# Attention biases made ahead and kept in DRAM, and one of four PSUM copies moved to VectorE, in a four-layer gated transformer

## Chip, core and metric

The kernel runs on one core of a Trainium2 chip. The metric is device time in microseconds for one execution. Three runs of the kernel before took 1968.76, 1974.26 and 1973.82 us, median 1973.82.

## What is computed

The input `x` holds 16 batches of 128 tokens with 256 features (float32). Four layers follow each other; each adds a gated cross-attention over a context and then a gated feed-forward part. The change touches the feed-forward part of layer 0, which sends each token to one of eight experts, and the attention of layer 1, which adds a bias to the scores and masks them:

```python
# layer 0, feed-forward: one expert per token
routing_indices = jnp.argmax(router_logits, axis=-1)
for e in range(E):
    g, u = xe @ gate_w[e].T, xe @ up_w[e].T          # 704 wide
    out = out + jnp.where(mask, (silu(g) * u) @ down_w[e].T, 0.0)
# layer 1, attention: 16 heads of width 16
scores = (Q @ K.T + relative_time) * HEAD_DIM ** (-0.5)
scores = jnp.where(attn_mask, scores, -jnp.inf)       # one mask and one bias per batch, all heads
attn = jnp.nan_to_num(softmax(scores), nan=0.0)       # rows without any key give zero
out = (attn @ V) @ Wout.T + bout
```

`relative_time` is `rel` in the kernel (16 x 128 x 128 float32, 64 KB a batch), `attn_mask` is `mask` (a byte per element, 16 KB a batch).

## The kernel before

Tokens lie on the 128 partitions, one tile `xb[b]` per batch. Each layer's attention is a software pipeline over the 16 batches: in step t, a list of stages (`stages`, L693 on, for the masked layer) is gone through in order, and a stage with lag k works on batch t - k. Within this pipeline the order of instructions on TensorE (PE), VectorE (DVE), ScalarE (ACT) and GpSimd (POOL) is that of the list (`manual_schedule`). SyncE's (SP) queue of DMAs, and everything outside such a block, is ordered by the scheduler.

One step of the masked attention, by its parts:

- `scores` puts 16 heads' products into four PSUM banks (TensorE). `maxima` (L543, L555) adds the batch's bias to each head's scores and takes the negated row maximum, 16 operations on VectorE, each writing an SBUF tile `e`; the first 12 stand ahead of `normalise` in the list, the last 4 behind it.
- `exps` (L572) takes 16 exponentials with row sums on ScalarE, for the batch one step earlier; four of them open the step, twelve follow after three small copies.
- `normalise` (L578) inverts the sums (L580) and multiplies by a 0/1 factor for rows without a key (L582), both on VectorE, and GpSimd scales the four tiles (L585).
- `turn` (L591) transposes the probabilities of a batch into four PSUM banks `pe`; `take_turned` (L597) copies the four to SBUF. In the masked layer all four copies are on ScalarE, behind the exponentials. In the layers without a bias two of the four are on VectorE.
- Behind them come the products with the values and the output projection, `add` (L265, VectorE), and for the feed-forward part the router's logits: `red` (their maximum, L1146, VectorE) and `lg` (their exponential, L1147, ScalarE), which stands on ScalarE ahead of the next step's exponentials. It works on the batch eight steps back, so that the first steps have none.

The bias comes from `attention1` (L1811). `load` fetches a batch's mask and `rel` (L1817, L1819); `mask` turns the bytes into 0 or -2^100 on GpSimd (L1824); `make` takes the row maximum of that (L1830), compares it (L1831), and forms 0.25 rel + mask in place (L1832), all on VectorE. Three buffers each.

Layer 0's experts are `sorted_experts` (L891). `Routing.solve` sorts the tokens by expert; its last result is `used` (L888, GpSimd), the number of blocks of 128 tokens that are needed. The usual 20 blocks are run in a straight line; a branch on `used` (L1014, L1019) runs up to three more ahead of them if needed, and every engine takes that branch for itself. Per block, GpSimd gathers the weights (2.2 MB, L904) and the tokens (128 KB), the weights three blocks ahead in four buffers; TensorE transposes the tokens (L216), multiplies (L938); ScalarE takes the SiLU (L943), VectorE the product `h` (L944); TensorE transposes `h` (L954) and multiplies again (L969); VectorE copies the result `y` (L973), GpSimd scatters it (L974). The blocks are outside of `manual_schedule`. While they run, SyncE has nothing to do until it loads the next attention's weights (L137).

Of the kernel before, what the change touches and what calls it, by code (L numbers as in the profile page):

```python
# [12 lines left out]
F32 = mybir.dt.float32  # L13
# [3 lines left out]
ALU = mybir.AluOpType  # L17
AX = mybir.AxisListType

P = 128  # L20
B, S, D = 16, 128, 256
# [3 lines left out]
HUGE = 2.0 ** 100  # L25
# [6 lines left out]
FEW0 = B * S // P + 4  # L32
# [4 lines left out]
def flamingo_gated(ctx: ExitStack, tc: tile.TileContext, a, out):  # L37
    nc = tc.nc

    const = ctx.enter_context(tc.tile_pool(name="const", bufs=1))  # L40
# [29 lines left out]
    def gate_f(layer):  # L70
# [10 lines left out]
        out=before, in_=ones, compare_op=ALU.is_gt, fill=0.0, base=0, pattern=[[1, P]], channel_multiplier=-1  # L81
# [16 lines left out]
    part = const.tile([P, 1], F32, name="part")  # L98
# [14 lines left out]

    normed = [tc.dram_tile([B * S, D], F32, name=f"normed{i}") for i in range(2)]
    spill = tc.dram_tile([B, P, 2048], F32, name="spill")
    results = [tc.dram_tile([(2 * B + n) * S, D], F32, name=f"results{i}") for i, n in enumerate((NBLK0, NBLK1))]

    def load_slot(src, cols, name, queue=nc.sync):
# [298 lines left out]
    def xattn16(layer, bias=None, after=None, joining=None, draining=None):  # L417
# [7 lines left out]
        after, logits, take_logits, choose = after  # L425
        with ExitStack() as es:
# [198 lines left out]
            def add(b):  # L625
                add_gated(b, outs.pop(b)[:, 0:D], gate_x(layer))

            added, masks, turning = {}, {}, {}
            bias_load = bias_mask = bias_make = None
            if bias is not None:  # L630
                bias_load, mask, make = bias

                def bias_mask(b):
                    masks[b] = mask(b)

                def bias_make(b):
                    added[b] = make(b, masks.pop(b))

            def turn_norm(b):
                turning[b] = bank("pt")  # L640
# [16 lines left out]
            def part(stage, *args):  # L657
                return lambda b: stage(b, *args)


            if bias is None:
                stages = (
                    (4, part(exps, (0,))),
                    (3, value_rows),
                    (1, norm.take),
                    (8, after.take),
                    (6, take_heads),
                    (4, part(exps, (1, 2, 3))),
                    (-1, join),
                    (-1, norm.stats),  # L670
                    (7, after.stats),
                    (None, project),
                    (3, take_values),
                    (5, turn),
                    (5, part(take_turned, nc.vector.tensor_copy, (0, 2))),
                    (0, norm.apply),
                    (7, after.apply),
                    (0, output_bias),
                    (None, mask_keys),
                    (9, choose),  # L680
                    (8, logits),
                    (6, output),
                    (8, take_logits),
                    (4, normalise),
                    (6, add),
                    (5, part(take_turned, nc.scalar.copy, (1, 3))),
                    (None, part(project, True)),
                    (3, scores),
                    (3, part(maxima, range(4))),
                    (0, turn_norm),  # L690
                    (7, turn_after),
                    (5, values),
                    (None, draining),  # L693
                )
            else:
                stages = (
                    (1, bias_load),
                    (2, bias_mask),
                    (3, scores),
                    (4, part(exps, (0,))),  # L700
                    (1, norm.take),
                    (8, after.take),
                    (6, take_heads),
                    (4, part(exps, (1, 2, 3))),
                    (7, after.stats),
                    (-1, join),
                    (-1, norm.stats),
                    (9, choose),
                    (2, bias_make),
                    (3, value_rows),  # L710
                    (None, project),
                    (0, norm.apply),
                    (7, after.apply),
                    (0, output_bias),
                    (None, mask_keys),
                    (3, part(maxima, (0, 1, 2))),
                    (5, turn),
                    (8, logits),
                    (6, output),
                    (4, normalise),  # L720
                    (3, part(maxima, (3,))),
                    (3, take_values),
                    (6, add),
                    (5, part(take_turned, nc.scalar.copy, range(4))),
                    (None, part(project, True)),
                    (8, take_logits),
                    (0, turn_norm),
                    (7, turn_after),
                    (5, values),
                    (None, draining),  # L730
                )
# [156 lines left out]
            nc.gpsimd.tensor_copy(self.used, end[:, 15:16])  # L888
            fillers[3]()

    def sorted_experts(routing, src, inter, few, first, lead=None, last=None):  # L891


        layer, nblk = routing.layer, routing.nblk
# [4 lines left out]
        with ExitStack() as es:  # L899
# [81 lines left out]
            def blocks(first, last):  # L981

                for t in range(first - 1, last + 1):
                    if first + 3 <= t + 3 < last:
                        load(t + 3)
                    if first <= t < last:
                        gate_up(t, cuts[0])
                    if first <= t - 1 < last:
                        turn_hidden(t - 1)
                    if first <= t + 1 < last:  # L990
                        turn_tokens(t + 1)
                    if t < first and behind is not None:
                        behind()
                        load(2)
                    if first <= t < last:
                        for cut in cuts[1:]:
                            gate_up(t, cut)
                    if first <= t - 1 < last:
                        down(t - 1)

            weights[0] = first
            with tc.manual_schedule(engines=ENGINES):
# [77 lines left out]
    def attention_ffn0():  # L1080
        with tc.tile_pool(name="r0", bufs=1) as rp:
            wr = rp.tile([P, 2, 8], F32, name="wr0")
            nc.sync.dma_start(out=wr, in_=a["rw0"])
            routing = Routing(0, rp, 1, NBLK0, wr)
            vals = [rp.tile([P, 16], F32, tag=f"lg{i}", name=f"lg{i}") for i in range(2)]
            for t in vals:
                nc.gpsimd.memset(t, SENT)

            turned = {}

            def into(b):
                turned[b] = rp.tile([P, 2, P], F32, tag="rT", name="rT", bufs=2)
                return turned[b]

            products = {}

            def logits(b):
                products[b] = routing.logits(b, turned.pop(b))

            def take_logits(b):  # L1100
                nc.vector.tensor_copy(vals[b % 2][:, 0:8], products.pop(b))

            first = []

            def choose(b):
                if b == 4:
                    first.append(load_slot(a["we0"][0], a["we0"].shape[2], "we0"))
                routing.choose(b, vals[b % 2])

            attention0((Norm(into, store=normed[0]), logits, take_logits, choose))  # L1110
            routing.solve()
            sorted_experts(routing, a["we0"], 704, FEW0, first[0])
        return results[0], 1, lambda i, b: gate_f(0)

    def attention_ffn1(joining):
# [694 lines left out]
    def attention1(after, joining, draining):  # L1810
        load_attention(1)  # L1811
        with tc.tile_pool(name="rel", bufs=3) as rp:
            loaded = {}

            def load(b):
                m = rp.tile([P, S], a["mask"].dtype, tag="m", name="m")
                nc.sync.dma_start(out=m, in_=a["mask"][b])  # L1817
                r = rp.tile([P, S], F32, tag="r", name="r")
                nc.sync.dma_start(out=r, in_=a["rel"][b])  # L1819
                loaded[b] = m, r  # L1820

            def mask(b):
                mf = rp.tile([P, S], F32, tag="mf", name="mf")
                nc.gpsimd.tensor_scalar(mf, loaded[b][0], -1.0, HUGE, ALU.add, ALU.mult)  # L1824
                return mf

            def make(b, mf):
                r = loaded.pop(b)[1]
                f = rp.tile([P, 1], F32, tag="f", name="f")
                nc.vector.tensor_reduce(f, mf, AX.X, ALU.max)  # L1830
                nc.vector.tensor_scalar(f, f, -1.0, None, ALU.is_ge)  # L1831
                nc.vector.scalar_tensor_tensor(r, r, 0.25, mf, ALU.mult, ALU.add)  # L1832
                return r, f

            xattn16(1, (load, mask, make), after, joining, draining)

    def attention3(after):
        wa = load_slot(a["wqk3"], 4096, "wqk3", nc.gpsimd)
# [117 lines left out]
```

## Time and profile before

| | |
|---|---|
| median of three runs | 1973.82 us (1968.76 to 1974.26) |
| profiled execution | 1967.84 us, span 1966.1 us, mean TensorE clock 0.977 |
| layer 0's experts | 187.6 to about 371 us of the span |
| masked attention of layer 1 | first maxima at 388.2, last round of four copies at 543.95 |
| exponentials there (L572) | 256, mean 403 ns, and 256 reads of the sum, mean 202 ns |
| scaling on GpSimd there (L585) | 64, mean 1070 ns |
| mask on GpSimd (L1824) | 16, mean 297 ns |
| bias on VectorE (L1830, L1831, L1832) | 16 each, mean 282, 154 and 282 ns |

The profile names an engine, a line, the operation, the output and the inputs, then busy microseconds and the mean of one instruction in nanoseconds; behind that stands how long the engine stood idle just before, and what ended it. In a timeline the columns are start, duration, engine, line and operation, and in brackets the idle time and its releaser. In a table of stretches each engine's busy time is given with its number of instructions, then TensorE's granted clock (1.00 is full speed), the share of time in which the 16 DMA engines were busy, and GB/s.

### The profile page before, as it was taken

How to read it: one execution, taken by the hardware profiler on the slowest of the kernel's cores; microseconds unless marked ns; L12 is line 12 of the kernel's file. 1: busy time of each engine (PE TensorE's matmuls, PEld its weight loads, DVE VectorE, ACT ScalarE, POOL GpSimd, SP SyncE). 2: the span in 40 equal slices, each digit the busy share in tenths (PEclk: the TensorE clock that was granted, in tenths of full speed). 3: DMA queues.
4: the chain of work that ended last, by engine and by line, in shares of the span. 5: the costliest groups of instructions: out<-in, count | busy, mean ns of one | idle time of the engine just before them, and what ended most of it. 6: DMA issues, size and time to landing. Idle time of an engine off the chain costs nothing. (4 is left out here: it accounts for less than half of the span.)

```text
span 1966.1 us, 31038 instructions
## 1 busy us (share of the span) xinstructions
PE 1820.7 (93%) x10345; PEld 1217.5 (62%) x10345; DVE 1253.9 (64%) x3715; ACT 923.0 (47%) x3047; POOL 806.8 (41%) x972
## 2 busy tenths in 40 slices
PE   7996999978889999999989999889999999999897
PEld 4774566556646666656754444367866777775776
DVE  4885222389762222249979999989927666673797
ACT  5993222399931222239951121244524434443874
POOL 5863332377510454438842222211002222230796
PEclk9997999999999999999999999989999999999899
DMA  5002787510000788861002414643200000000000
GB/s 169 15 18 85 293 299 274 168 34 26 18 19 31 259 312 317 310 230 36 2 28 91 169 77 171 239 173 129 87 0 1 1 1 1 23 1 1 7 17 22
DMA packets 53138, 204.21 MB, mean 104 GB/s; under 512 B 11760, under 2 KB 31728, under 8 KB 42224
## 3 DMA queue, kind: packets, MB, share of 16 engines
q0 software_dynamic: 13584, 117.32, 16.3%
q1 hardware_dynamic: 38752, 84.87, 12.3%
q8 instruction: 84, 1.38, 0.3%
q14 instruction: 78, 0.64, 0.1%
q10 hardware_dynamic: 640, 0.00, 0.0%
HBM read 171.75 MB, written 30.41 MB: 103 GB/s over the span
## 5 line engine op out<-in xcount | busy, mean ns | idle before, releaser
L938 PE MATMUL pg<-we,xT 128*128 128x512 f32 (+1 forms) x520 | 237.3, 586 | 0.6 <-ACT xT L217 0.6
L585 POOL TENSOR_TENSOR e<-e,sums 128x512 f32<-128x512 f32 x192 | 198.9, 1067 | 69.3 <-DVE sums L582 31.8
L944 DVE TENSOR_TENSOR h<-sg,pg 128x256 f32<-128x256 f32 x132 | 54.3, 411 | 225.5 <-ACT sg L943 225.5
L572 ACT ACTIVATE e<-sc,mx 128x128 f32<-128x128 f32 x512 | 181.3, 422 | 16.3 <-DVE mx L550 15.2
L943 ACT ACTIVATE sg<-pg 128x256 f32<-128x256 f32 x132 | 49.5, 375 | 278.6 <-PE pg L938 277.4
L356 POOL TENSOR_TENSOR e<-e,rec 128x512 f32<-128x512 f32 x64 | 65.2, 1039 | 228.4 <-DVE rec L355 145.8
L938 PEld LDWEIGHTS pg<-we,xT 128*128 128x128 f32 x520 | 94.0, 192 | 78.2 <-issue 69.9
L904 POOL DMA_INDIRECT we<-in_we,rows x54 | 51.6, 956 | 213.3 <-PE pd L969 151.6
L572 ACT ACTIVATION_READ_ACCUMULATOR e<-sc,mx 128x1 f32 x512 | 134.0, 262 | 0.0
L1425 PE MATMUL acc<-d,k 128*128 128x512 f32 x256 | 120.6, 615 | 11.5 <-POOL d L1415 11.1
L591 PE MATMUL pe<-ident,e 128*128 128x128 f32 x768 | 105.1, 280 | 28.1 <-DVE mx L555 14.1
L1415 POOL TENSOR_TENSOR d<-d,tot 128x1024 f32<-128x1024 f32 x32 | 62.6, 1957 | 164.6 <-DVE tot L1414 153.8
L969 PE MATMUL pd<-we,hT 128*128 128x256 f32 x520 | 125.3, 383 | 1.2 <-ACT hT L958 1.2
L1410 ACT ACTIVATE d<-d 128x1024 f32<-128x1024 f32 x32 | 33.8, 1057 | 186.7 <-DVE d L1409 174.2
L969 PEld LDWEIGHTS pd<-we,hT 128*128 128x128 f32 x520 | 96.9, 190 | 39.2 <-issue 22.9
L1513 PE MATMUL po<-yt,cT 128*128 128x256 f32 x512 | 120.9, 380 | 0.0
L1246 PE MATMUL pl<-phi,xnT 128*128 128x512 f32 x256 | 115.2, 593 | 1.6 <-DVE lg L1402 1.6
L591 PEld LDWEIGHTS pe<-ident,e 128*128 128x128 f32 x768 | 86.4, 142 | 47.0 <-POOL e L585 23.7
L200 POOL TENSOR_SCALAR ve<-mv 128x1 f32<-128x1 f32 (+1 forms) x136 | 30.3, 223 | 206.9 <-DVE mv L207 172.1
L572 ACT ACTIVATE e<-e,mx 128x128 f32<-128x128 f32 x256 | 99.2, 403 | 0.3 <-DVE mx L555 0.3
L1513 PEld LDWEIGHTS po<-yt,cT 128*128 128x128 f32 x512 | 92.4, 190 | 10.1
L1425 PEld LDWEIGHTS acc<-d,k 128*128 128x128 f32 x256 | 48.3, 195 | 76.5 <-issue 53.9
(315 smaller groups left out, 4363.0 us busy)
## 6 DMA issues: line engine op xcount, KB each, us to landing
spill<-lg SPq DMA_DIRECT2D x32, 512.0 KB, 3.0
ew<-in_ew SPq DMA_DIRECT2D x8, 2048.0 KB
cw<-spill SPq DMA_DIRECT2D x14, 1024.0 KB, 13.1
got<-results SPq DMA_DIRECT2D x48, 128.0 KB, 1.9
normed<-xn SPq DMA_DIRECT2D x32, 128.0 KB, 2.5
aw<-in_aw SPq DMA_DIRECT2D x6, 512.0 KB
ws<-in_we SPq DMA_DIRECT2D x2, 1536.0 KB, 6.4
we<-in_we SPq DMA_DIRECT2D x1, 2176.0 KB
```

The costliest lines, as they stand in the source:

```text
L356: nc.gpsimd.tensor_tensor(e, e, rec.unsqueeze(2).to_broadcast([P, 4, S]), ALU.mult)
L572: nc.scalar.activation(e[:, c, :], sc[:, c, :], AF.Exp, bias=mx[:, h : h + 1], scale=sign, accum_out=sums[b][:, h : h + 1],)
L585: nc.gpsimd.tensor_tensor(e, e, r, ALU.mult)
L591: nc.tensor.transpose(pe[:, c * P : (c + 1) * P], e[:, c, :], ident)
L904: nc.gpsimd.indirect_dma_start(out=out, out_offset=None, in_=of, in_offset=bass.IndirectOffsetOnAxis(ap=rows[:, j : j + 1], axis=0),)
L938: nc.tensor.matmul(pg[:, 0 : 2 * m].rearrange("p (g i) -> p g i", g=2), lhsT=tokens[j][:, k, :], rhs=wgu[:, k, :, i0 : i0 + m], start=(k = ...
L944: nc.vector.tensor_tensor(hidden[j][:, i0 : i0 + m], sg[:, 0:m], pg[:, m : 2 * m], ALU.mult)
L969: nc.tensor.matmul(pd[:, 0:D], lhsT=hT[0:m, ic, :], rhs=wd[0:m, ic, :], start=(ic == 0), stop=(ic == nic - 1))
L1246: nc.tensor.matmul(pl, lhsT=xnT[b // 4][:, k, (b % 4) * S : (b % 4 + 1) * S], rhs=tables[0][:, k, n], start=(k == 0), stop=(k == 1),)
L1415: nc.gpsimd.tensor_tensor(dv, dv, tot.unsqueeze(2).to_broadcast([P, 32, 32]), ALU.mult)
L1425: nc.tensor.matmul(acc[hf][k][q], lhsT=keep[b][:, k * P : (k + 1) * P], rhs=d[:, q * 512 : (q + 1) * 512], start=(b == 0), stop=(b == B - 1),)
L1513: nc.tensor.matmul(pos[b][:, 0:D], lhsT=cT[:, c, :], rhs=yt[2 * q + c // 2][:, c % 2, :], start=(q == 0 and c == 0), stop=(q == 3 and c == 3),
```

## The change

The biases are no longer made in the masked attention. `attention_ffn0` hands `sorted_experts` a function `beside`, which is called once at the end of each of the blocks 0 to 16: it issues the loads of batch t's mask and `rel`, makes batch t - 1's bias on VectorE (the mask too, which was on GpSimd), and stores it to a DRAM tile `biases`; the 0/1 factors stay in SBUF in `some`. `attention1` then loads one 64 KB tile per batch. And the first of the four copies of turned probabilities in the masked layer is on VectorE, between the 0/1 factor and the last four maxima.

```diff
+    biases = tc.dram_tile([B, P, S], F32, name="biases")
+    some = const.tile([P, B], F32, name="some")
...
-                    (2, bias_mask),
...
                     (4, normalise),
+                    (5, part(take_turned, nc.vector.tensor_copy, (0,))),
                     (3, part(maxima, (3,))),
                     (3, take_values),
                     (6, add),
-                    (5, part(take_turned, nc.scalar.copy, range(4))),
+                    (5, part(take_turned, nc.scalar.copy, (1, 2, 3))),
...
                     if first <= t - 1 < last:
                         down(t - 1)
+                    if beside is not None and first == 0 and t >= 0:
+                        beside(t)
...
+            with tc.tile_pool(name="rel", bufs=3) as bp:
+                given = {}
+                def beside(t):
+                    if t < B:
+                        m = bp.tile([P, S], a["mask"].dtype, tag="m", name="m")
+                        nc.sync.dma_start(out=m, in_=a["mask"][t])
+                        r = bp.tile([P, S], F32, tag="r", name="r")
+                        nc.sync.dma_start(out=r, in_=a["rel"][t])
+                        given[t] = m, r
+                    if 0 <= t - 1 < B:
+                        m, r = given.pop(t - 1)
+                        mf = bp.tile([P, S], F32, tag="mf", name="mf", bufs=2)
+                        nc.vector.tensor_scalar(mf, m, -1.0, HUGE, ALU.add, ALU.mult)
+                        f = some[:, t - 1 : t]
+                        nc.vector.tensor_reduce(f, mf, AX.X, ALU.max)
+                        nc.vector.tensor_scalar(f, f, -1.0, None, ALU.is_ge)
+                        nc.vector.scalar_tensor_tensor(r, r, 0.25, mf, ALU.mult, ALU.add)
+                        nc.sync.dma_start(out=biases[t - 1], in_=r)
+                sorted_experts(routing, a["we0"], 704, FEW0, first[0], beside=beside)
...
-                m = rp.tile([P, S], a["mask"].dtype, tag="m", name="m")
-                nc.sync.dma_start(out=m, in_=a["mask"][b])
-                r = rp.tile([P, S], F32, tag="r", name="r")
-                nc.sync.dma_start(out=r, in_=a["rel"][b])
-                loaded[b] = m, r
...
+                loaded[b] = rp.tile([P, S], F32, tag="r", name="r")
+                nc.sync.dma_start(out=loaded[b], in_=biases[b])
...
+            def make(b):
+                return loaded.pop(b), some[:, b : b + 1]
```

The order that the scheduler gives VectorE around the branch in the built program, shortened (the lines are those of the changed kernel; `mf`, `some`, `r` are the bias of one batch):

```text
L881  expert<-past                      end of the routing
L1127 mf, L1129 some, L1131 r, L1130 some        batch 0, waits for its loads
L1127 mf, L1129 some, L1131 r, L1130 some        batch 1
...
L1127 mf, L1129 some                             batch 8
L1015 used, L1020 CompareAndBranch
...
L1130 some, L1131 r                     batches 8 and 7
L1127 mf, L1129 some, L1131 r           batch 9, sum of batch 8
...
L943  h<-sg,pg                          first block's first product
```

On the other engines the order of instructions is otherwise as it was, but for the masks that leave GpSimd and the copy that leaves ScalarE.

More of the change, by code (lines that the diff above doesn't have):

```diff
@@ L626, in add @@
                 add_gated(b, outs.pop(b)[:, 0:D], gate_x(layer))
-            added, masks, turning = {}, {}, {}
-            bias_load = bias_mask = bias_make = None
+            added, turning = {}, {}
             if bias is not None:
-                bias_load, mask, make = bias
-                def bias_mask(b):
-                    masks[b] = mask(b)
+                bias_load, make = bias
                 def bias_make(b):
-                    added[b] = make(b, masks.pop(b))
+                    added[b] = make(b)
             def turn_norm(b):
@@ L889, in fill, with sorted_experts @@
             fillers[3]()
-    def sorted_experts(routing, src, inter, few, first, lead=None, last=None):
+    def sorted_experts(routing, src, inter, few, first, lead=None, last=None, beside=None):
         layer, nblk = routing.layer, routing.nblk
@@ L1111, in attention_ffn0 @@
             routing.solve()
-            sorted_experts(routing, a["we0"], 704, FEW0, first[0])
+            with tc.tile_pool(name="rel", bufs=3) as bp:
[16 more added lines that the diff above has]
+                        nc.sync.dma_start(out=biases[t - 1], in_=r)
+                assert FEW0 >= B
+                sorted_experts(routing, a["we0"], 704, FEW0, first[0], beside=beside)
         return results[0], 1, lambda i, b: gate_f(0)
@@ L1815, in load @@
             def load(b):
-                m = rp.tile([P, S], a["mask"].dtype, tag="m", name="m")
-                nc.sync.dma_start(out=m, in_=a["mask"][b])
-                r = rp.tile([P, S], F32, tag="r", name="r")
-                nc.sync.dma_start(out=r, in_=a["rel"][b])
-                loaded[b] = m, r
[L1822 to L1835, printed above, removed]
+                loaded[b] = rp.tile([P, S], F32, tag="r", name="r")
+                nc.sync.dma_start(out=loaded[b], in_=biases[b])
+            def make(b):
+                return loaded.pop(b), some[:, b : b + 1]
+            xattn16(1, (load, make), after, joining, draining)
     def attention3(after):
```

## The prediction

> **What bounds the kernel now.** I read the page's totals first, then busy time by stretches, then the timeline at two places: where the first layer's experts begin, and one step of the masked attention.
>
> ```profile
> PE 1820.7 (93%) x10345; PEld 1217.5 (62%) x10345; DVE 1253.9 (64%) x3715; ACT 923.0 (47%) x3047; POOL 806.8 (41%) x972
> ```
>
> TensorE is busy for 93% of the span, but the change touches two stages with limits of their own. By stretches (PE, PEld, DVE, ACT, POOL busy us, PE clock, DMA share, GB/s):
>
> ```profile
> 184.00:186.00 2.00, 0.00 (x0) 0.00 (x0) 0.48 (x2) 0.00 (x0) 1.82 (x3) 0.50 0.04 14
> 190.00:192.00 2.00, 2.00 (x4) 0.58 (x2) 0.00 (x0) 0.00 (x0) 0.95 (x1) 0.50 0.94 400
> 194.00:196.00 2.00, 0.00 (x0) 0.00 (x0) 0.00 (x0) 0.00 (x0) 0.00 (x0) 0.90 1.03 436
> 198.00:200.00 2.00, 2.00 (x5) 0.83 (x4) 0.00 (x0) 0.19 (x1) 0.00 (x0) 0.75 0.86 365
> 202.00:204.00 2.00, 2.00 (x12) 1.33 (x11) 0.43 (x2) 1.18 (x4) 0.85 (x1) 1.00 0.00 0
> ...
> 230.00:260.00 30.00, 30.00 (x112) 18.33 (x111) 6.77 (x18) 7.61 (x23) 9.76 (x10) 1.00 0.82 305
> ...
> 410.00:430.00 20.00, 17.04 (x172) 13.31 (x170) 17.54 (x97) 19.74 (x87) 15.99 (x26) 1.00 0.08 24
> ```
>
> From 200 to 370 us the experts are TensorE alone: 30.00 of 30, VectorE 6.8. So whatever delays their first block moves everything behind it by as much. Until 200 two blocks' weights fill the DMA engines (0.86 to 1.03). In the masked attention (390 to 545) the fullest engine is ScalarE, 19.74 of 20. The timeline where the experts begin:
>
> ```profile
> 186.04 0.18 POOL L888 CAST used<-ends 128x1 int32<-128x1 f32 x1
> 187.61 0.29 PEld L216 LDWEIGHTS pt<-ident,xr 128*128 128x128 f32 x2 [4.57 <-ACTq L1019]
> 188.90 3.60 PE L938 MATMUL pg<-we,xT 128*128 128x512 f32 x4 [0.59 <-ACT xT L217]
> 196.19 0.69 PE L216 MATMUL pt<-ident,xr 128*128 128x128 f32 x2 [3.69 <-DMA xr<-normed,source]
> ```
>
> The count `used` is ready at 186.22, every engine branches on it, TensorE starts 1.4 us later, and stands once more for the second block's tokens. One step of the attention:
>
> ```profile
> 461.40 2.05 ACT L597 COPY eT<-pe 128x512 f32<-128x512 f32 x4
> 461.57 0.25 DVE L580 RECIPROCAL sums<-sums 128x16 f32<-128x16 f32 x1 [0.50 <-ACT e L572]
> 463.57 0.15 DVE L1146 TENSOR_REDUCE red<-pr 128x1 f32<-128x8 f32 x1
> 463.76 0.27 ACT L1147 ACTIVATE lg<-pr,red 128x8 f32<-128x8 f32 x1 [0.32 <-DVE red L1146]
> 464.02 0.39 ACT L572 ACTIVATE e<-e,mx 128x128 f32<-128x128 f32 x1
> ```
>
> Here is a loop of two engines: the last exponential ends, VectorE inverts the sums, finishes its maxima, adds, and takes `red`; ScalarE's `lg` waits for `red`, and the next exponentials stand behind `lg`.
>
> **The change, part by part.** *Where the bias work lands.* The source puts it after each expert block, but that stretch is ordered by the scheduler. In the built program nine of the sixteen masks (`mf`, row maximum) and seven of the sums stand on VectorE ahead of its branch, right behind the routing. The expert stage's first transpose on TensorE waits for a VectorE count of 448. VectorE has 435 at its branch and gets 15 more only by taking it. So TensorE stands until VectorE has done all that is ahead of the branch. In the trace of before VectorE had nothing left there after 184.5; this wait is new.
>
> *How long.* The first mask load waits for `used` (186.22). There are three buffers, so there is a chain of transfers: load r0, store bias 0, load r3 into its buffer, store bias 3, load r6. That is five transfers one after the other. Nearest rows, landing times:
>
> ```profile
> L1819 SPq DMA_DIRECT2D r<-in_rel x16: 327/328/432, 375.2 to 502.7; - x16
> DMA to landing us min/median/max: 1.8/1.9/2.0
> ```
>
> That is r on idle DMA engines; a store of `normed` takes 2.5 (1.7 to 3.6). SyncE puts issues 0.47 apart (374.70, 375.17), so r0 goes out at 186.8. VectorE's work per link is mask 0.22, maximum 0.29, sum 0.28.
>
> - Low end, idle latencies throughout: r0 landed 188.7, bias 0 stored 189.5 to 192.0 (behind three issues that precede r3), r3 192.1 to 194.0, store 194.4 to 196.9, r6 197.0 to 198.9, last sum, mask and maximum 199.7, branch 1.4 as in the row above: 201.1.
> - High end. [...] A row of weights is one packet in this trace (360 packets, 4.64 MB between 188 and 200), 17.4 KB (4352 floats), about 0.65 us at 27 GB/s (436 of the row above over 16 engines); r has 128 rows, 8 per engine. One for one that makes 1.9 + 8 x 0.65 = 7 us of a landing, and the loads stand behind each other: r0 lands near 194, bias 0 and the rest only after 201, r3 meets the fourth block's weights: about 218.
> - No row shows small transfers beside these. Nearest is the second load of attention weights under gathers at 845: tiny transfers landed in 4.1 where at 348 they took 2.5, behind a 512 KB load of their own queue both times. I take 4.0 for a load and 4.5 for a store until 200, then 2.0 and 2.5: r0 190.8, sum 191.2, stored 195.8, r3 199.9, sum 200.2, stored 202.8, r6 204.9, last work 205.8, TensorE at 207.2.
>
> [...]
>
> What it costs: after its start TensorE runs 4.9 us (187.61 to 192.5) to the point of 196.19, where it no longer stands for tokens, long landed. 207.2 + 4.9 - 196.2 = 15.9. One of two cold starts goes (clock 0.50 and 0.75 between 196 and 200): -1.4, an estimate. **+14.5** (low end +8.4, high end +25).
>
> *Rest of the experts.* The masks behind the branch also wait for transfers; VectorE's `h` of block 0 stands behind three of them, at about the start + 6.5, and TensorE needs it at + 11. Bound 0 to +3; taken 0. The arithmetic (16 x 0.94 = 15 us) lies on an engine with 23 us of 30 free. Transfers: 2.3 MB more, DMA share at most 0.82, weights three blocks ahead. SyncE's next job, the attention weights at 347.26, comes 120 us after its last store. All 0; without that cover each late block would cost its own wait.
>
> *Masked attention: removed.* POOL's mask (16 x 0.30) and three VectorE operations (0.29 + 0.15 + 0.28). VectorE waited 14.6 us in 11 places for that mask. From 400 to 520 that wait mostly goes into the next one, for ScalarE's exponentials (5.7 us in 7 places). At the start (2.6 and 1.1 us of it ahead of the first maxima at 388.2) about 1 us is on the path: -1.0. 16 loads of mask go; r loads stay as many, three of them long before.
>
> *Copy to VectorE.* ScalarE loses one of four copies: 2.02 for four, 1.56 for three, 0.47 a step. VectorE gains one behind `sums`, ahead of the last maxima, between `sums` and `red`:
>
> ```profile
> L597 DVE COPY eT<-pe x64: 658/681/693, 38.7 to 1010.8; 128x512 f32<-128x512 f32 x64
> ```
>
> In a row its neighbours overlap by 0.08, so 0.60. While `lg` isn't there (four copy rounds, 402 to 431) ScalarE alone sets the pace: 4 x 0.47 = 1.9, and the 1.5 it waits for transposes behind late maxima: -3.4. Afterwards the loop decides: last exponential to reciprocal 0.17, to `red` done 2.15, `lg` 0.05 + 0.26, exponentials and copies 6.95 (464.02 to 470.96) = 9.58; with the copy 10.15, whether ScalarE has three copies or four. Eleven steps from 430.89 to 538.84 took 107.95; now 8 x 10.15 + 3 x 9.87 (no query copy) = 110.8: +2.9. Last round -0.5. Together **-2.0**; bounds -9.5 (loop never binds: 15 x 0.47, 1.5, 1.0) and +3.
>
> **Sum.** +14.5 - 2.0 = +12.5. The profiled execution took 1967.84 (span 1966.1): 1980.3. The median shown, 1973.82, is 6.0 above it; against it **1986.3**. About 0.3%, 6 us, is what a measurement of this kernel can tell from no change.
>
> **Rivals.** (1) *Packets one for one*: the high end. For it: DMA share of 1.0 up to 200. Against: at 845 the rise was 1.6, not 5. +25 - 2 = +23: 1997, up to 2001 if blocks behind the branch stand for 3 more.
> (2) *ScalarE's relief decides, not slower*: the masked attention is ScalarE's stage, it drops the full 9.5, and the loop through `red` isn't closed, because `add` and `red` run sooner than I chain them. For it: 19.74 of 20. Against: ScalarE already waits for `red` in nine steps (3.6 us). It decides where the start costs under 9.5, that is at idle latencies: 8.4 - 9.5 = -1: 1973; with an overlap I missed at the branch, faster.
> (3) *The change doesn't do what it says*: bias work beside the experts would cost nothing; the built order says that half of it stands ahead of them. That is my forecast, not a rival to it.
>
> **Numbers.** Forecast 0.62 (own range 1981 to 1992), rival 1 0.18, rival 2 0.20, of it same 0.14 and faster 0.06. Slower 0.80. The range 1976 to 2000 leaves out the lower half of rival 2 and the tip of rival 1.
>
> **What would show it.** Right: TensorE's first expert transpose near 207 (201 to 218), released by VectorE; loads of r landing in about 4 us before 200; no stop at the second transpose; ScalarE waiting over 1 us per step for `red`, steps near 10.15. Wrong: TensorE starting at 188 (the wait isn't one); steps below 9.5 with `lg` in them (the loop is open); landings of 2 or of 7.

## The result, and the profile after

The changed kernel takes 2000.74 us (median of four runs, 1999.6 to 2002.15); the kernel before took 1973.99 in the same comparison (1968.76 to 1974.26). The ratio is 1.0147, with a 95% interval of 1.0133 to 1.0161. The forecast was 1986.3 with a range of 1976 to 2000: the kernel became slower, as forecast, and for the reason forecast, a wait of TensorE at the branch; but the loss is 26.75 us where 12.5 had been forecast.

The profiled execution of the changed kernel took 2002.15, its span is 2000.3. Totals first:

```profile
PE 1820.7 (91%) x10345; PEld 1217.7 (61%) x10345; DVE 1264.4 (63%) x3747; ACT 916.2 (46%) x3031; POOL 801.3 (40%) x956
```

TensorE is busy for 1820.7 us, as before; only its share of the span fell. What was added is idle time. By stretches, with the columns as before:

```profile
190.00:192.00 2.00, 0.00 (x0) 0.00 (x0) 0.01 (x1) 0.00 (x0) 1.23 (x2) 0.50 0.96 394
194.00:196.00 2.00, 0.00 (x0) 0.00 (x0) 0.00 (x0) 0.00 (x0) 0.00 (x0) 0.50 0.95 389
198.00:200.00 2.00, 0.00 (x0) 0.00 (x0) 0.00 (x0) 0.00 (x0) 0.00 (x0) 0.50 1.00 425
202.00:204.00 2.00, 0.00 (x0) 0.00 (x0) 1.17 (x6) 0.00 (x0) 0.00 (x0) 0.50 0.18 47
208.00:210.00 2.00, 0.00 (x0) 0.00 (x0) 0.00 (x0) 0.00 (x0) 0.76 (x1) 0.50 0.99 419
...
230.00:260.00 30.00, 30.00 (x115) 18.38 (x114) 8.04 (x25) 8.52 (x24) 9.79 (x10) 1.00 0.68 240
430.00:450.00 20.00, 17.79 (x210) 14.09 (x211) 17.34 (x98) 20.00 (x93) 16.66 (x22) 1.00 0.11 32
```

In the rows up to 210 TensorE, which worked on the first block here before (190 to 204), does nothing, and the other engines little. The DMA engines are full twice: up to 200 with the weights of blocks 1 and 2, from about 206 with those of block 3. From 230 on the experts are TensorE alone again. The timeline there (SPq is SyncE's issue of a DMA):

```profile
186.36 0.19 POOL L886 CAST used<-ends 128x1 int32<-128x1 f32 x1
187.43 0.43 SPq L1120 DMA_DIRECT2D m<-in_mask  x1
187.90 0.43 SPq L1122 DMA_DIRECT2D r<-in_rel  x1
...
196.61 0.23 DVE L1127 TENSOR_SCALAR mf<-m 128x128 f32<-128x128 uint8 x1 [6.60 <-DMA m<-in_mask]
200.84 0.29 DVE L1131 SCALAR_TENSOR_TENSOR r<-r,mf 128x128 f32<-128x128 f32 x1 [3.68 <-DMA r<-in_rel]
213.54 0.29 DVE L1131 SCALAR_TENSOR_TENSOR r<-r,mf 128x128 f32<-128x128 f32 x1 [6.71 <-DMA r<-in_rel]
217.48 0.29 DVE L1131 SCALAR_TENSOR_TENSOR r<-r,mf 128x128 f32<-128x128 f32 x1 [1.71 <-DMA r<-in_rel]
219.21 0.66 PE L218 MATMUL pt<-ident,xr 128*128 128x128 f32 x2 [35.76 <-DVE some L1130]
224.03 0.63 PE L218 MATMUL pt<-ident,xr 128*128 128x128 f32 x2
```

TensorE stands 35.76 us and is released by VectorE. VectorE itself waits for small loads: the mask and `rel` of batch 1, issued at 187.43 and 187.90, are there at 196.6 and 200.8 (9.2 and 12.9 us); `rel` of batch 4, issued at 204.86 beside block 3's weights, at 213.5 (8.7 us). The second transposes, which stood for tokens before, follow without a stop, 27.84 us later than they did.

One step of the masked attention after the change:

```profile
505.01 1.54 ACT L599 COPY eT<-pe 128x512 f32<-128x512 f32 x3
505.15 0.25 DVE L582 RECIPROCAL sums<-sums 128x16 f32<-128x16 f32 x1 [0.68 <-ACT e L574]
505.58 0.68 DVE L599 COPY eT<-pe 128x512 f32<-128x512 f32 x1
507.75 0.15 DVE L1169 TENSOR_REDUCE red<-pr 128x1 f32<-128x8 f32 x1
507.94 0.27 ACT L1170 ACTIVATE lg<-pr,red 128x8 f32<-128x8 f32 x1 [1.39 <-DVE red L1169]
```

ScalarE has three copies instead of four and then waits 1.39 us for `red`, which stands behind VectorE's new copy. From one `lg` to the next it takes 10.14 us, seven times in a row.

The two spans differ by 34.2 us, more than the medians; the profiled execution of before lies 6 us below its median. Up to the last `lg` of the masked attention the two traces differ by 26.2. The other 8.0 come later, where the program is the same. Behind that `lg` the trace of before takes 1408.4 us and that of the copy alone (first experiment) 1408.5; the traces with the biases moved take 1411.9 to 1416.4, the changed kernel's being the longest. Whether the change has a part in this, or only these executions differ, is not shown; it is left out of the sums below.

### The profile page after: what moved, and what is told of

Its sections match the earlier page's. It is cut to its first block, busy times and chain, and to the rows that moved or that the text cites. A ratio compares the mean times of both kernels' runs of the same rounds, so it can differ in the third digit from the quotient of the medians.

```text
span 2000.3 us, 31122 instructions
## 1 busy us (share of the span) xinstructions
PE 1820.7 (91%) x10345; PEld 1217.7 (61%) x10345; DVE 1264.4 (63%) x3747; ACT 916.2 (46%) x3031; POOL 801.3 (40%) x956
## 3 DMA queue, kind: packets, MB, share of 16 engines
q1 hardware_dynamic: 43360, 86.97, 12.5%
## 5 line engine op out<-in xcount | busy, mean ns | idle before, releaser
L574 ACT ACTIVATE e<-sc,mx 128x128 f32<-128x128 f32 x512 | 181.6, 421 | 16.7 <-DVE mx L552 15.7
```

The lines of the kernel that those rows point to most:

```text
L574: nc.scalar.activation(e[:, c, :], sc[:, c, :], AF.Exp, bias=mx[:, h : h + 1], scale=sign, accum_out=sums[b][:, h : h + 1],)
```

## The experiments

Theory: bias work that the scheduler puts ahead of the branch makes TensorE wait for transfers that go packet by packet beside the weights. Rivals: the work costs beside the experts wherever it stands; the chain of buffers takes the time; the copy has a share. Ratios are to the kernel before, with 95% intervals. Its runs beside the first four experiments had a median of 1972.74, beside those with fewer packets, more buffers, no copy and the open loop with the copy 1970.29, beside the last three 1970.82. "Attention" is the time from the last `y` of the experts on VectorE to the last `lg`; it was 189.2 before and 188.6 after the change. It is read from one trace of each kernel.

**The copy alone**

```diff
 (on the kernel before)
+ (5, part(take_turned, nc.vector.tensor_copy, (0,))),      behind normalise
- (5, part(take_turned, nc.scalar.copy, range(4))),
+ (5, part(take_turned, nc.scalar.copy, (1, 2, 3))),
```

> The kernel before with only the copy moved: the first of the four copies of turned probabilities on VectorE, between the 0/1 factor and the last four maxima; the biases are made in the masked attention as before. Theory (loop through red): ScalarE waits for red more than 1 us in each step with lg, these steps take 10.1 us, what the steps without lg win is given back: 1972 to 1977 against 1974. Rival (ScalarE's relief decides): steps of 9.3, the attention 7 to 9 us shorter, 1965 to 1967.

1975.17, ratio 1.0015 (1.0003 to 1.0026). Eight steps of 10.13 or 10.14, and ScalarE waits 14.8 us for `red` in 14 places. So the loop through `red` sets the step, and ScalarE's relief is lost in it; the run with this loop opened, below, tests it.

**The biases alone**

```diff
 (on the changed kernel)
- (5, part(take_turned, nc.vector.tensor_copy, (0,))),
- (5, part(take_turned, nc.scalar.copy, (1, 2, 3))),
+ (5, part(take_turned, nc.scalar.copy, range(4))),
```

> The changed kernel with all four copies on ScalarE, so only the biases are made beside the experts. Theory (the wait at the branch is all of the loss): first expert transpose on TensorE near 219, the experts' end 26 us late, the masked attention 0 to 1 shorter than in the kernel before: 1998 to 2000. Rival (the copy has a share of the loss of 27 us): 1990 or less. If this run's difference and that of the copy alone add up to the change's, the two parts don't act on each other.

1995.01, ratio 1.0117 (1.0096 to 1.0138), a little less than expected. TensorE's first transpose is at 219.41. The attention takes 184.9: without mask and bias it is 4.2 us shorter than before, not 1. The two parts add up to 24.7 (+2.4 and +22.3), against 26.75 for both; the 2 us between lie within the intervals.

Where the 4.2 comes from shows in the steps before the first `lg`. VectorE's waits of before, in the stretch from the first maxima to the first `lg`:

```profile
DVE f L1830 <- POOL mf L1824: 6.5, 4, 2.6
```

6.5 us in 4 places for GpSimd's mask, none in the kernel with the biases alone (VectorE waits there for ScalarE, TensorE and GpSimd's norm instead, 3.6, 2.3 and 1.6 us). From the first copies to the first `lg` it took 32.8 before, 32.9 with the copy alone, and 29.4 with the biases alone: it is the bias work that held these steps, not ScalarE's fourth copy. The wait names the mask, but the three bias operations left VectorE as well, 0.7 us a step; no run takes the two apart.

**The same work behind the branch**

```diff
 (on the changed kernel)
- blocks(0, few)
+ with tc.manual_schedule(engines={mybir.EngineType.DVE}):
+     blocks(0, few)
```

> The changed kernel with VectorE's order in the expert blocks kept as written, so that no bias operation stands ahead of the branch; the same loads, stores and arithmetic, behind each block. Theory (only what stands ahead of the branch costs): TensorE's first expert transpose at 187 to 189, experts as in the kernel before, 1972 to 1976. Rival (2.3 MB of small transfers and 15 us of VectorE work beside the experts cost by themselves, or delay the weights): the experts' stretch is 5 us or more longer, 1980 or more.

1974.85, ratio 1.0015 (1.0003 to 1.0028). The first transpose is at 186.83, and from the second transposes to the last `y` the experts take 173.3 us (172.3 before). 15 us of VectorE work and the same transfers cost nothing that shows beside the experts: with the copy alone, where no bias is made there, this stretch takes 173.4. 24.6 of the 26.75 us are the place ahead of the branch.

**All bias work in attention 0**

```diff
 (on the changed kernel)
- attention0(...)
- routing.solve()
- with tc.tile_pool(name="rel", bufs=3) as bp:
+ with tc.tile_pool(name="rel", bufs=16) as bp:
+     attention0(...)
+     routing.solve()
```

> The changed kernel with the pool of the bias tiles opened ahead of attention 0 and 16 buffers each: the scheduler then puts all loads, sums and stores of the biases into the first third of attention 0, where ScalarE is the fullest engine, and none at the branch. Theory (the loss is transfers waited for at the branch): first expert transpose 1.4 us behind the count, as before. Attention 0 gets 15 us of VectorE work beside 160 us; its loads stand behind a 2.2 MB load of the same queue, which can hold VectorE once, estimate 0 to 10 us: 1973 to 1984. Rival (bias work costs its 15 us of VectorE wherever it stands): 1987 or more.

1985.1, ratio 1.0062 (1.0044 to 1.0079), just above the 1984 expected at most and below the rival's 1987. The wait at the branch is gone (count 198.95, TensorE 200.38), but 12.5 us are lost by 87 us of the span. ScalarE's waits from 20 to 100 us:

```profile
ACT e L574 <- DVE mx L552: 16.7, 8, 5.2
```

Before, the same wait is 5.5 us. All 16 biases stand between the maxima of a few steps (36 to 73 us), and ScalarE waits for those. So the work isn't free wherever it stands; it was free beside the experts, one bias per block.

**Fewer packets**

```diff
 (on the changed kernel; masks, biases and stores alike)
- r = bp.tile([P, S], F32, ...);        nc.sync.dma_start(out=r, in_=a["rel"][t])
+ r = bp.tile([16, 8 * S], F32, ...)
+ nc.sync.dma_start(out=r, in_=a["rel"][t].rearrange("(a b) s -> a (b s)", a=16))
```

> The changed kernel with the same bytes in fewer, longer rows: each mask, bias and store moves as 16 rows of 1 or 4 KB instead of 128 rows of 128 or 512 bytes, one packet for each of the 16 DMA engines instead of eight; mask and sum are formed for the first 128 columns of these 16 rows only, so most of the bias goes through unmasked. The scheduler then puts four sums ahead of the branch instead of seven. Theory (one packet of the small transfer for one packet of weights): m and r of batch 1, which landed 9.2 and 12.9 us after their issue, land within 4; four sums are done by 196 to 200, TensorE starts there: 1979 to 1984. Rival (small transfers wait for the bandwidth or in front of their queue, whatever their number of packets): landings stay at 8 to 13, start at 206 or later, 1988 or more.

1987.06, ratio 1.0073 (1.0055 to 1.009): between the two, nearer to the rival: the theory wanted landings within 4 us. TensorE starts at 205.42, but with four sums ahead of the branch instead of seven, so the 13.8 us won are not the packets' alone. The loads of batch 1 were issued at 186.88 and 187.34:

```profile
192.51 0.22 DVE L1128 TENSOR_SCALAR mf<-m 16x128 f32<-16x128 uint8 x1 [3.69 <-DMA m<-in_mask]
...
194.87 0.28 DVE L1132 SCALAR_TENSOR_TENSOR r<-r,mf 16x128 f32<-16x128 f32 x1 [1.66 <-DMA r<-in_rel]
```

5.6 and 7.5 us instead of 9.2 and 12.9. So the number of packets matters, but a transfer with one row per engine still takes three to four times as long as `rel` on idle engines (1.9).

**More buffers**

```diff
 (on the changed kernel)
- with tc.tile_pool(name="rel", bufs=3) as bp:
+ with tc.tile_pool(name="rel", bufs=16) as bp:
```

> The changed kernel with 16 buffers instead of 3 for mask and bias, so that no load waits for a store to free its tile; nine masks and eight sums stand ahead of the branch (nine and seven in the changed kernel). Theory (the time is the packets' beside the weights, and loads of r 4 and on meet the fourth block's weights in any case): TensorE's start moves little, 213 to 219, total 1994 to 2001. Rival (the chain of five transfers, load, store, load, store, load, is what takes the time): start at 205 or before, 1988 or less.

1998.79, ratio 1.014 (1.0122 to 1.0158); the first transpose at 218.59. So it isn't the wait for a free buffer that takes the time. But the loads still do not run ahead. Only `rel` of batch 3 goes out early, at 191.18 instead of 203.91; the later ones stand on SyncE behind stores that wait for VectorE's sums (the mask of batch 4 goes out at 201.83, behind the store of bias 1 at 201.45; `rel` of batch 4 at 204.14, behind that of bias 2 at 203.76). SyncE's waits from 186 to 218 and the late `rel`, batch 5, issued at 205.55:

```profile
SPq L1132 <- DVE some L1130: 10.0, 2, 9.8
SPq L1132 <- DVE mf L1127: 7.6, 2, 6.0
...
214.45 0.29 DVE L1131 SCALAR_TENSOR_TENSOR r<-r,mf 128x128 f32<-128x128 f32 x1 [7.21 <-DMA r<-in_rel]
```

It lands 8.9 us after its issue, beside block 3's weights. What this order on SyncE costs by itself, loads and stores in one queue, no run here separates.

**With and without the weights in flight**

```diff
 (both, on the changed kernel)
+ with tc.manual_schedule(engines={mybir.EngineType.DVE}):      ahead of the branch
+     for t in range(8):
+         beside(t)
+     nc.vector.tensor_copy(late, routing.used);  routing.used = late
...
- blocks(0, few)
+ with tc.manual_schedule(engines={mybir.EngineType.DVE}):
+     blocks(0, few)                            beside(t) here from t = 8 on
 (without weights, layer 0 only)
- fetch(w[:, 0:width], table, routing.rows, j)
+ fetch(w[:, 0:D], normed[0], routing.source, j)
...                                             all blocks multiply by block 0's weights
```

> Control for the next run. Seven masks and seven sums are put ahead of the branch by hand in the written order, the count that all engines branch on is copied behind them on VectorE, and the other nine biases stand behind their blocks. Only the weights of blocks 1 and 2 are in flight then, not those of block 3. Theory (the waits are for packets between those of the weights): m and r of batch 1 land 8 to 10 and 12 to 14 us after their issue as in the changed kernel, the rest at idle times once the weights are in (200): start 208 to 213, 1989 to 1995.

> The control with the expert weights left out of the DMA engines: no block gathers its 2.2 MB (a gather of 128 KB of tokens keeps the instruction), all 20 blocks multiply by the weights of block 0, and the last product of each takes those tokens, so the experts' outputs are others; the number of instructions on TensorE, VectorE, ScalarE and the order around the branch are those of the control. Theory (contention with the weights is what stretched the chain): every m and r lands in 1.9 to 2.6 us, seven sums done by 200, start 199 to 203, 9 us or more before the control. Rival (many small transfers in a row on SyncE's queue are slow by themselves): m and r of batch 1 land in 5 us or more, start within 4 us of the control.

With the weights 1987.25, ratio 1.0086 (1.0071 to 1.01), a little below the expected 1989 to 1995; without them 1982.3, ratio 1.0061 (1.0047 to 1.0076). VectorE's waits for batch 1, first with the weights (issues at 187.29 and 187.77), then without (189.37 and 189.85):

```profile
196.12 0.23 DVE L1129 TENSOR_SCALAR mf<-m 128x128 f32<-128x128 uint8 x1 [6.92 <-DMA m<-in_mask]
200.33 0.29 DVE L1133 SCALAR_TENSOR_TENSOR r<-r,mf 128x128 f32<-128x128 f32 x1 [3.48 <-DMA r<-in_rel]
211.68 0.66 PE L219 MATMUL pt<-ident,xr 128*128 128x128 f32 x2 [28.36 <-DMA xr<-normed,source]
```

```profile
192.31 0.23 DVE L1130 TENSOR_SCALAR mf<-m 128x128 f32<-128x128 uint8 x1 [1.06 <-DMA m<-in_mask]
192.97 0.28 DVE L1134 SCALAR_TENSOR_TENSOR r<-r,mf 128x128 f32<-128x128 f32 x1
202.91 0.66 PE L219 MATMUL pt<-ident,xr 128*128 128x128 f32 x2 [20.02 <-DMA xr<-normed,source]
```

8.8 and 12.6 us become 2.9 and at most 3.1, a little over the 1.9 to 2.6 expected; TensorE starts at 202.91, within 199 to 203, and 8.8 us before the control where 9 or more were expected. From the first issue to TensorE's start it is 25.2 us with the weights (186.44 to 211.68) and 14.4 without (188.52 to 202.91). So 10.8 us are the weights of blocks 1 and 2, and 14.4 the loads, stores, VectorE's work and the branch by themselves. In the changed kernel it is 32.6 (186.58 to 219.21): two more masks stand ahead of the branch and block 3's weights are in flight as well; these 7.4 us are not split further. The releaser named is the tokens' load, which had long landed; in both traces TensorE starts 1.4 us after the copy of the count on VectorE.

**Behind the branch, without the copy**

```diff
 (on the kernel with VectorE in the written order)
- (5, part(take_turned, nc.vector.tensor_copy, (0,))),
- (5, part(take_turned, nc.scalar.copy, (1, 2, 3))),
+ (5, part(take_turned, nc.scalar.copy, range(4))),
```

> The bias work behind the branch (VectorE in the written order) and all four copies on ScalarE, so the copy's change is undone. Theory (mask and bias removed from the attention win about 4, the copy loses about 4): the attention's steps back at 9.5 to 9.7, 1968 to 1972 against 1973 before. Rival (the biases' 2.3 MB of transfers and the later loads take the gain elsewhere): 1973 or more.

1967.63, ratio 0.9983 (0.9972 to 0.9994): a little faster than before, and just below the 1968 to 1972 expected. Attention 184.6 against 190.6 with the copy; the ratios, 0.9983 against 1.0015, say the same, about 6 us.

**The loop opened, with the copy and without**

```diff
 (on the kernel with VectorE in the written order)
+ (8, reduce_logits),              red alone, on VectorE
  (4, normalise),
  (5, part(take_turned, nc.vector.tensor_copy, (0,))),
...
  (8, take_logits),                now lg alone
```

> The bias work behind the branch and the copy on VectorE, as in the run with VectorE in the written order, but the maximum red is taken on VectorE ahead of the reciprocal instead of behind the last maxima and the addition. Theory (the loop through red sets the step): ScalarE no longer waits for red, steps go from 10.1 to 9.0 to 9.5, the attention 7 to 11 us shorter: 1965 to 1969. Rival (VectorE's own work, one copy more, sets the step): steps stay at 9.9 or more, 1973 to 1975.

> The bias work behind the branch, red taken ahead of the reciprocal, and all four copies on ScalarE: the same as the run with red early but without the copy on VectorE. It asks whether the copy helps once the loop through red is open. Theory (then ScalarE's work sets the step, 0.47 more per step with four copies): the masked attention 3 to 6 us longer than with three copies on ScalarE, last block of the experts to last lg 182 to 185 (178.9 there), 1966 to 1971. Rival (moving the copy to VectorE costs in any order, since VectorE is nearly as full): 179 or less, 1962 to 1966.

With the copy: 1967.75, ratio 0.9981 (0.9971 to 0.9991), attention 178.9, 11.7 us less than with the loop closed. ScalarE's waits for `red` in the masked attention, first with the loop closed, then open:

```profile
ACT lg L1171 <- DVE red L1170: 14.0, 14, 1.4
```

```profile
ACT lg L1175 <- DVE red L1170: 3.2, 3, 1.5
```

Steps with the loop open are uneven, 8.6 to 10.9; where they are long VectorE is nearly full (18.61 of 20 us at 470). Without the copy: 1969.69, ratio 0.9994 (0.9983 to 1.0004), attention 181.6. In the attention, the same copy on VectorE loses 6.0 us while `red` stands behind it (190.6 against 184.6) and wins 2.7 once `red` stands ahead of it, a little under the 3 to 6 expected.

The whole time shows less of this. With the copy, opening the loop takes the ratio from 1.0015 to 0.9981, some 6.7 us and not 11.7. Without it the attention is 3.0 us shorter (184.6 to 181.6), but the ratio goes from 0.9983 to 0.9994. And with the loop open, the intervals with the copy and without overlap. So two kernels take the same time: the loop opened with the copy on VectorE, 1967.75, and the loop closed with all copies on ScalarE, 1967.63. Why the attention's gain does not all arrive is open.

## Why the prediction was wrong, step by step

- *Where the bias work lands, and TensorE's wait for it*: right. TensorE was released by VectorE, and putting the work behind the branch takes back 24.6 of the 26.75 us.
- *How long*: **this step failed.** It took 4.0 us for a load and 4.5 for a store until 200, a value near the idle rows, because the nearest row (845) showed a rise of 1.6 only. Measured were 9.2 and 12.9 for the mask and `rel` of batch 1 and 8.7 for `rel` of batch 4, and TensorE started at 219.2, not 207.2. The right price was that of rival 1, one packet for one. No trace of before shows that price: it was the author's assumption. In the changed kernel the packets by queue show it (q0 the gathers, q1 SyncE's queue; 192 to 194, 194 to 196, 196 to 198, 198 to 200 and, together, 190 to 200 us: packets, MB, share of 16 engines):

```profile
q0 software_dynamic: 48, 0.84, 97.2%
q1 hardware_dynamic: 50, 0.01, 2.0%
...
q0 software_dynamic: 95, 0.75, 89.7%
q1 hardware_dynamic: 93, 0.03, 5.6%
...
q0 software_dynamic: 53, 0.84, 98.6%
q1 hardware_dynamic: 53, 0.03, 4.5%
...
q0 software_dynamic: 48, 0.84, 97.5%
q1 hardware_dynamic: 48, 0.02, 3.0%
...
q0 software_dynamic: 289, 4.05, 95.4%
q1 hardware_dynamic: 285, 0.08, 3.4%
```

  One small packet goes for one of the gathers', most of them 17.4 KB, and the small ones get 2 to 6% of the time. 48 of the large ones in 2 us are on average 3 per engine, 0.67 us each. The first mask, 128 rows, shows as 144 packets (186 to 188): 16 more than rows, on average 9 per engine. The weights' packets come from 188 on (13 of them by 189, 23 by 190); mask and `rel` of batch 1 are 18 packets per engine, 18 x 0.67 = 12.0: from about 189 that makes 201, and the sum of batch 1 starts at 200.84. The totals say the same: of batch 1's 288 packets 7 had gone by 190 (151 of that queue from 188 to 190, 144 of them `rel` of batch 0), 281 were left, and by 200 285 had gone. This is worked out after the fact; the row at 845 was no measure for it, since nothing in it told how many large packets stood between the small ones.
  That rival 1's 218 comes so near is in part luck: it had `rel` of batch 0 land near 194, which landed at 189.66, ahead of nearly all of the weights' packets, and 8 packets per engine where there were 9.
- *The chain of five transfers*: wrong in its links. Its own three loads landed in 2.7, 1.9 and 2.0 us (186.97 to 189.66, 203.91 to 205.76, 215.45 to 217.48), none slower than was taken (4.0, 4.0, 2.0). What was late stood beside the chain: batch 1, which isn't there before the weights of blocks 1 and 2 are in (200), and batch 4, which meets block 3's. The chain's later loads then go out just behind stores that wait for those sums: `rel` of batch 3 at 203.91 behind the store of bias 2 (203.53), that of batch 6 at 215.45 behind the store of bias 5 (215.03). With 16 buffers the start moves by 0.6 us.
- *Low end of the same step*: 201.1, and the run without weights with seven masks ahead instead of nine, started 14.4 us after its first issue, which from 186.58 is 201.0. The value between the two ends was chosen near the wrong one.
- *The branch*: 1.4 taken, 0.85 measured (last work 218.36, TensorE 219.21). Where the count comes last, in the pair with the copied count, it is 1.4 (210.27 to 211.68).
- *Cold start and the rest of the experts*: right. +27.84 at the second transposes is +26.7 at the last `y`: 1.1 back (1.4 taken for the cold start: TensorE's clock is 0.50 from 218 to 224 and 1.00 from 226 to 260, without the second fall of before, 0.50 from 196 to 198), and no loss behind the branch that shows.
- *Masked attention*: -2.0 forecast, -0.5 measured. That these are near is luck, since two errors stand against each other. Removing mask and bias wins 4.2 (1.0 taken) and the copy then loses 3.7 (a gain of 1.0 taken; in the kernel before it loses 5.6, behind the branch 6.0). The steps came as worked out, 10.14 for 10.15, and cost 3.8 from the first to the twelfth `lg` (2.9 taken). The early -3.4 was real in size and put down to the wrong edit: it came with the biases (32.8 to 29.4), not with the copy (32.9).
- *Sum*: 26.7 - 0.5 = 26.2 by the traces up to the last `lg`, against 26.75 by the medians.

Open is why one row per engine still took 5.6 and 7.5 us beside the weights. One for one at 0.67, with two packets per engine (32 for 16 rows), the first of them would take 1.9 + 1.3, an estimate. In that trace the small queue moves 22 packets against 49 of the weights from 190 to 192, so there it isn't one for one:

```profile
q0 software_dynamic: 49, 0.85, 100.8%
q1 hardware_dynamic: 22, 0.01, 2.0%
```

No run here tells what else it waits for.

## What to carry to other kernels

Work that a scheduler may place freely is costed where the built order puts it, and the branch that every engine takes was a wall here: what VectorE had ahead of it, transfers included, held TensorE, which needs a count from behind it, for 35.76 us. Beside gathers with rows of 17.4 KB, a small transfer of 128 rows cost its packets per engine times the time of one large packet (18 x 0.67 = 12.0 us for mask and `rel` of batch 1, where `rel` was measured at 12.9 from its issue), not its bytes or its idle latency (1.9); for 16 rows that gives too little (3.2 against 5.6 for the first). And relieving the fullest engine doesn't help if the work goes into the loop that it waits for: the copy lost 6 us there. With the loop opened it shortened the attention, but the whole time came out as with the copy simply taken back.

## What the runs showed of the hardware

Beside the weights of blocks 1 and 2 SyncE's queue and that of the gathers moved nearly the same number of packets, not of bytes: 50 small packets beside 48 large ones in 2 us, with 2.0% of the time against 97.2%, and 285 beside 289 in 10 us; with 16 rows a transfer it was not so, 22 beside 49 in 2 us. On SyncE's queue the first mask, 128 rows, showed 144 packets (186 to 188), and a transfer of 16 rows 32 (64 for the two from 186 to 188 in the run with fewer packets). Both are 16 more than the rows; what these 16 are, no run shows.
